# Earlier raw context loads and x loads in the second layer's cross attention of a four-layer transformer

## The chip, the cores and the metric

The kernel runs on 1 core of a Trainium2 chip. The metric is the device time of one execution in microseconds; the median of the runs is what versions are compared by.

## The reference

`x` is (32, 112, 256), `ctx` is (32, 375, 256). Four layers are run one after another on `x`; each attends to the same `ctx`:

```
x = L0(x, ctx)   # x attends to ctx: 16 heads of 64, 4 key heads
x = L1(x, ctx)   # self attention, cross attention, GELU-gated feed-forward
x = L2(x, ctx)   # cross attention with 16 heads of 64, ReLU feed-forward
x = L3(ctx, x)   # causal self attention, cross attention, ReLU feed-forward
```

The second layer's cross attention is what the change touches. It has 16 heads of 16, and its queries, keys, values and attention weights are quantised to 8 bits:

```
h2  = layernorm(x)
q, k, v = h2 @ wq, ctx @ wk, ctx @ wv
sim = einsum(fq(q), fq(k)) * DH**-0.5
out = einsum(fq(softmax(sim)), fq(v))
x   = out @ wo + bo + x
```

## The kernel before, in words

**Sweeps, units and slots.** The work is cut into nine sweeps over the 32 batches: `l0x`, `l1s`, `l1x`, `l1f`, `l2x`, `l2f`, `l3s`, `l3x`, `l3f` (the digit is the layer; s, x and f are self attention, cross attention and feed-forward). Sweeps run in pairs side by side: `l0x` with `l1s`, `l1x` with `l1f`, `l2x` alone, `l2f` with `l3s`, `l3x` with `l3f`. A sweep consists of units; in `l1x` a unit is one batch, and two batches share a layer norm. A unit has slots; in `l1x` eight, each with one pair of heads. `order` merges the slots of all sweeps into one list, and `run` goes through it slot by slot.

**What a slot of `l1x` does.** A slot has steps that come some slots after one another (`LAGS`: 0, 1, 3, 6, 7 for `l1x`). Step 0 makes the scores on TensorE (L1166) and the softmax (`softmax`: maximum L640 on VectorE, scaled maximum L643 and exponential L646 on ScalarE). One slot later the probabilities are scaled and rounded (`quant_p`: L215 on VectorE or GpSimd, L691 on VectorE) into a bf16 tile. Three slots later, in every second slot, a DMA transposes that tile (L1185). Six slots later TensorE multiplies by the values (L1130). Seven slots later, at the last slot of a unit, comes the output projection with the residual sum (L1267).

**Atoms.** Everything else a unit needs is an atom: a piece of work with a lead in slots of its own sweep, a cost on TensorE, and a function. The atoms of a sweep are sorted by the slot they are due in. `settle` runs those without a cost as soon as their slot begins; `fill` spreads those with a cost over the slots before, up to `HORIZON` slots ahead, but never past an atom without a cost that isn't due yet. The leads stand in `LEAD`; a lead of 14 means fourteen slots before the unit's first slot. For `l1x`: `load` and `stats` and `apply` are the load of x, the layer norm's statistics (L460 to L462, L435) and its application (L475, transposes L477); `cload` and `cut` are described next; `q` and `k` are the query and key projections with their quantisation (L213, L949, L970); `apart` spreads queries over heads (L935); `v` makes the values (L1018, L1030); `v2` makes the values of the third layer from the same context and stores them in DRAM as `vd` (L536); `again` loads x a second time for the residual.

**The context in `l1x`.** `ctx_atoms` has two atoms a batch. `load` (`cload`) takes a `k3` tile, has GpSimd clear one column (L574) and issues the DMA of the transposed context, 375 KB (L575). `cut` takes a `k6` tile and splits the raw context into a high and a low part: the copy of the high part goes to ScalarE (L202) and VectorE (L204) in turn, batch by batch, the subtraction to GpSimd (L233). The result is stored as `cd` (L586) for the later sweeps.

**Queues and buffers.** All DMAs are issued by SyncE (SP), in one order. Loads of x (L405), stores of x (L430) and stores of `vd` are held back by `later` and let go by `behind`, right behind the next DMA transpose of `l1x`. Tiles of one tag share a number of buffers: `k3` has 11 (in `l1x`: raw context, probabilities, their bf16 form, its transpose, values, vd tiles), `k6` 5, `x` 11. The instructions that the loop emits are then put in each engine's order when the program is built, by readiness, priority in the order of emission and free buffers; on the chip every engine takes its instructions in that order.

**Beside it.** `l1f` runs in the same stretch, one unit of eight slots for two batches: up projections (L1294), gate shift (L224), GELU on ScalarE (L1311), gating (L1323), down projections (L1334), residual (L866).

Of the kernel before, what the change touches and what calls it, by code (L numbers as in the profile page):

```python
# [61 lines left out]
class Kern:  # L62
# [7 lines left out]
        l1x=[0, 1, 3, 6, 7],  # L70
# [8 lines left out]
    LEAD = dict(  # L79
        l0x=dict(load=11, stats=10, apply=6, cload=11, cstats=8, cut=8, ctrans=5, q=4, k=[2, -2], v=-1),  # L80
        l1s=dict(load=5, stats=5, apply=3, q=2, k=2, v=1),
        l1x=dict(load=17, stats=12, apply=10, cload=14, cut=14, q=8, apart=[2, -1], k=4, v=-1, v2=[-2, -4, -6, -7], again=-7),
        l1f=dict(load=13, stats=11, apply=10, gate=2, gelu=1, again=-3),
        l2x=dict(load=10, stats=7, apply=6, cload=11, cut=7, q=4, k=[1, 1], v=0, vload=2),
        l2f=dict(load=6, stats=5, apply=3),
# [1583 lines left out]
```

## Time and profile before

| | us |
|---|---|
| median of three runs (4796.98, 4806.71, 4807.12) | 4806.71 |
| the profiled execution | 4799.79 |
| its span, first to last instruction | 4797.7 |
| PE busy | 4449.6 (93%) |
| VectorE (DVE) busy | 3619.7 (75%) |
| ScalarE (ACT) busy | 3412.9 (71%) |
| GpSimd (POOL) busy | 2131.3 (44%) |
| mean granted clock of TensorE | 0.968 |
| first and last raw context load of `l1x` | 1090.3 and 2149.5 |

How to read it: PE is TensorE's matrix multiplication, PEld its weight load. A wait row reads "who <- what ended the wait: us in total, times, longest". In the order of time a row gives the start, the duration, the engine, the line, the operation, the tiles out<-in, shapes, and in brackets the idle time of the engine just before, with what ended it. SPq is SyncE's queue of DMA issues; its durations are those of the issue, not of the transfer. Buffer numbers are left out of tile names, so that `k3` and `k6` both read `k`. The windows' columns are the busy time of each engine in that stretch, then the granted clock of TensorE as a share, the busy share of the DMA engines and GB/s.

### The profile page before, as it was taken

To read this page: it belongs to the slowest core of one execution; us is meant where nothing else is said; L and a number is where in the kernel's file an instruction comes from. 1 tells how busy PE (TensorE), PEld (TensorE's weight loads), DVE (VectorE), ACT (ScalarE), POOL (GpSimd) and SP (SyncE) were. 2 spreads that over 40 slices of the span, in tenths; PEclk is the share of its full clock that TensorE was granted. 3 is DMA by queue.
4 is the path that set the end of the run, shared out by engine and by line. 5 is a ranking of instruction groups with operands and counts; after the bars stand their busy time and mean duration, and the time that the engine had idled before them with its cause. 6 is when DMAs were issued, how large, how long until landed. Compare 5 with 4: busy or idle time off the path is not lost.

```text
span 4797.7 us, 111165 instructions
## 1 busy us (share of the span) xinstructions
PE 4449.6 (93%) x37824; PEld 3960.6 (83%) x37824; DVE 3619.7 (75%) x9803; ACT 3412.9 (71%) x10645; POOL 2131.3 (44%) x3676
## 2 busy tenths in 40 slices
PE   7999999998778999999999999999999997899999
PEld 6888888887667888887999999998899986778888
DVE  5788888888888888887688888888566655677776
ACT  5788888887767777775577777775555554677776
POOL 5455455556444343333233333334444443566665
PEclk9999999999889999999999999999999997899999
DMA  4433333334665565566355445543777777666663
GB/s 109 125 87 88 82 86 82 83 84 120 139 132 136 147 144 147 145 153 160 108 144 144 138 140 140 146 142 103 198 218 220 221 201 207 159 165 166 164 166 84
DMA packets 590020, 674.50 MB, mean 141 GB/s; under 512 B 331488, under 2 KB 499664, under 8 KB 589264
## 3 DMA queue, kind: packets, MB, share of 16 engines
q1 hardware_dynamic: 589456, 667.38, 54.6%
q8 instruction: 305, 5.00, 0.5%
q14 instruction: 259, 2.12, 0.1%
HBM read 323.55 MB, written 173.02 MB: 104 GB/s over the span
## 4 chain that ended last, share of the span: by engine, by line
PE 42%; DVE 5%; DMA 4%; ACT 1%; issue 1%; POOL 1%; SPq 0%; ACTq 0%; DVEq 0%; POOLq 0%
PE ps L698 7%; PE ps L237 6%; PE ps L238 5%; PE ps L239 5%; PE sc L807 3%; PE ps L829 3%; PE ps L1130 3%; PE sc L1166 2%; PE acc L237 2%; PE acc L239 1%; PE acc L238 1%; PE ps L1294 1%; DVE sm L640 1%; PE ps L1240 1%; DMA k<-k 1%
## 5 line engine op out<-in xcount | busy, mean ns | idle before, releaser
L219 POOL TENSOR_SCALAR k<-k,sm 112x375 f32<-112x375 f32 (+1 forms) x1536 | 941.7, 626 | 1054.1 <-DVE sm L680 474.5
L202 ACT ACTIVATE k<-ps 125x336 f32<-125x336 f32 (+4 forms) x2005 | 916.3, 470 | 419.8 <-PE ps L239 185.2
L640 DVE TENSOR_REDUCE sm<-sc 112x1 f32<-112x375 f32 x1792 | 945.1, 539 | 150.7 <-PE sc L807 86.6
L646 ACT ACTIVATE k<-sc,sm 112x375 f32<-112x375 f32 x1536 | 881.9, 580 | 103.3 <-DVE sm L640 79.9
L698 PE MATMUL ps<-ident,k 112*125 112x112 f32 x4608 | 736.4, 278 | 20.4 <-issue 4.0
L698 PEld LDWEIGHTS ps<-ident,k 112*125 112x125 f32 x4608 | 653.5, 191 | 76.0 <-issue 45.7
L807 PE MATMUL sc<-k,qs 128*112 128x376 f32 x2048 | 540.7, 357 | 21.4 <-ACT k L646 11.4
L237 PE MATMUL ps<-w,k 128*125 128x256 f32 (+2 forms) x1344 | 426.3, 317 | 32.0 <-ACT k L646 17.4
L729 DVE TENSOR_TENSOR k<-ps,k 64x376 fp32r<-64x376 f32 x640 | 350.3, 547 | 121.7 <-ACT k L202 106.5
L237 PE MATMUL ps<-h,w 128*128 128x224 f32 x1408 | 408.8, 297 | 34.6 <-DVE h L204 13.0
L204 DVE COPY k<-ps 125x336 f32<-125x336 f32 (+2 forms) x619 | 289.7, 468 | 152.3 <-PE ps L239 60.2
L238 PE MATMUL ps<-h,w 128*128 128x224 f32 x1408 | 394.0, 282 | 2.6 <-POOL h L233 2.0
L239 PE MATMUL ps<-h,w 128*128 128x224 f32 x1408 | 393.2, 282 | 1.3 <-POOL w L233 1.2
L238 PE MATMUL ps<-w,k 128*125 128x256 f32 (+2 forms) x1344 | 385.6, 287 | 0.0
L239 PE MATMUL ps<-w,k 128*125 128x256 f32 (+2 forms) x1344 | 384.7, 286 | 0.0
L829 PE MATMUL ps<-k,k 125*64 125x112 f32 (+1 forms) x4608 | 351.9, 297 | 1.6 <-ACT k L202 1.3
L215 POOL TENSOR_SCALAR k<-k,sm 112x375 f32<-112x375 f32 x256 | 165.8, 648 | 416.8 <-DVE sm L680 314.9
L237 PE MATMUL ps<-k,w 128*128 128x376 f32 x896 | 336.5, 376 | 15.2 <-ACT k L646 5.8
L807 PEld LDWEIGHTS sc<-k,qs 128*112 128x112 f32 x2048 | 305.3, 177 | 50.7 <-ACT k L646 24.9
L237 PEld LDWEIGHTS ps<-w,k 128*125 128x125 f32 (+2 forms) x1344 | 258.8, 193 | 82.5 <-ACT k L646 30.3
L646 ACT ACTIVATION_READ_ACCUMULATOR k<-sc,sm 112x1 f32 x1536 | 323.7, 211 | 0.0
L237 PEld LDWEIGHTS ps<-h,w 128*128 128x128 f32 x1408 | 272.4, 197 | 56.8 <-issue 18.2
(216 smaller groups left out, 12559.6 us busy)
## 6 DMA issues: line engine op xcount, KB each, us to landing
qs<-h SPq DMA_DIRECT2D x512, 224.0 KB
k<-k SPq DMA_DIRECT2D x192, 376.0 KB
k<-cd SPq DMA_DIRECT2D x64, 752.0 KB
vd<-k SPq DMA_DIRECT2D x128, 375.0 KB
k<-vd SPq DMA_DIRECT2D x128, 375.0 KB
qs<-dq_l3s SPq DMA_DIRECT2D x128, 224.0 KB
qs<-dq_l3x SPq DMA_DIRECT2D x128, 224.0 KB
x<-xd SPq DMA_DIRECT2D x224, 112.0 KB
```

What stands on the lines that cost most here:

```text
L202: self.nc.scalar.activation(out, in_, AF.Identity)
L204: self.nc.vector.tensor_copy(out, in_)
L219: self.nc.gpsimd.tensor_scalar(out, in_, by, 1.0, ALU.mult, ALU.mult)
L237: mm(out, lhs(0), rhs(0), start=start, stop=False)
L238: mm(out, lhs(0), rhs(1), start=False, stop=False)
L239: mm(out, lhs(1), rhs(0), start=False, stop=stop)
L640: nc.vector.tensor_reduce(nms[j], sc[j][:, :n], AX.X, ALU.max, negate=True)
L646: nc.scalar.activation(p[:, j, :n], sc[j][:, :n], AF.Exp, bias=nms[j], scale=1.0 if scale is None else scale, accum_out=sm[:, j : j + 1])
L698: self.nc.tensor.transpose(pst[:TB, a * S : (a + 1) * S], p[:, j, a * TB : (a + 1) * TB], self.ident[:S, :S])
L729: nc.vector.tensor_tensor(ks[o, j, :], pk[r, :TE], ks[r, j, :].bitcast(F32), ALU.subtract)
L807: nc.tensor.matmul(sc[:, :TE], qs[:, hd, q, bs], kk, start=q == 0, stop=q == 1)
L829: nc.tensor.matmul(o if gqa else o[:, mm, :], vq[:, a, hd * 64 : hd * 64 + 64], st["pt"][:, :, j, ta] if gqa else st["pt", mm][:, j, ta], ...
```

## The change

Two leads of `l1x` are altered. The load of x is emitted 20 slots ahead of its unit and not 17, its statistics still 12 slots ahead. The load of the raw context is emitted 16 slots ahead and not 14, while its split stays at 14, so that the two no longer fall in the same slot. No operation is added or removed.

```
     LEAD = dict(
         ...
-        l1x=dict(load=17, stats=12, apply=10, cload=14, cut=14, q=8, apart=[2, -1], k=4, v=-1, v2=[-2, -4, -6, -7], again=-7),
+        l1x=dict(load=20, stats=12, apply=10, cload=16, cut=14, q=8, apart=[2, -1], k=4, v=-1, v2=[-2, -4, -6, -7], again=-7),
```

## The prediction

> **What bounds the kernel now.** I read the page first, then the busy times by stage, then the raw context load with its waiters, then the order of time around one split. All numbers are of the profiled execution: 4799.79 us, span 4797.7 us, so 2.1 us lie around the span. The median of the runs shown is 4806.71 us, 6.9 us above it.
>
> ```profile
> span 4797.7 us, 111165 instructions
> PE 4449.6 (93%) x37824; PEld 3960.6 (83%) x37824; DVE 3619.7 (75%) x9803; ACT 3412.9 (71%) x10645; POOL 2131.3 (44%) x3676
> ...
> PE   7999999998778999999999999999999997899999
> ...
> PEclk9999999999889999999999999999999997899999
> ```
>
> PE is the engine nearest its limit, and it is loosest, with a lowered clock, in slices 10 to 13 (about 1080 to 1560 us). That is where `l1x` begins beside the tail of `l1s`. The raw loads (L575) run from 1090.3 to 2149.5 us, one a batch, some 33 us apart in the steady part, so a slot of `l1x` is about 4.2 us there. Only this stage is touched. Its first part, its steady part, and then 13 us around the split of an even and of an odd batch, in turn, three times:
>
> ```profile
> 1090.00:1500.00 410.00, 326.63 (x2446) 269.50 (x2445) 346.44 (x966) 298.58 (x903) 193.67 (x335) 0.86 0.59 132
> 1500.00:2160.00 660.00, 609.49 (x4643) 533.25 (x4642) 552.72 (x1517) 501.81 (x1360) 255.15 (x394) 0.98 0.61 147
> 1727.00:1740.00 13.00, 9.38 (x66) 7.73 (x66) 9.95 (x30) 7.14 (x16) 3.91 (x6) 0.87 0.77 169
> 1761.00:1774.00 13.00, 12.43 (x96) 10.12 (x95) 10.30 (x29) 9.48 (x29) 6.28 (x8) 1.00 0.63 168
> 1793.00:1806.00 13.00, 10.38 (x73) 8.70 (x72) 10.69 (x32) 8.29 (x17) 4.52 (x6) 0.87 0.74 178
> 1827.00:1840.00 13.00, 13.00 (x103) 11.34 (x102) 10.02 (x29) 9.73 (x29) 6.13 (x8) 1.00 0.62 161
> 1591.00:1604.00 13.00, 10.21 (x71) 8.64 (x70) 8.87 (x25) 7.56 (x18) 3.81 (x5) 0.84 0.86 194
> 1627.00:1640.00 13.00, 12.99 (x103) 11.50 (x102) 10.22 (x31) 10.10 (x30) 6.41 (x8) 1.00 0.59 161
> ```
>
> The columns are PE, PEld, DVE, ACT and POOL busy, granted clock, DMA share and GB/s. In the even windows PE is idle for 3.62, 2.62 and 2.79 us at a clock of 0.84 to 0.87; in the odd ones for 0.57, 0 and 0.01 us at full clock. Something happens every second batch. The split's first half falls on ACT in even and on DVE in odd batches, and this is who waits for the raw load in the whole run (us, times):
>
> ```profile
>   ACT k L202: 24.6, 13
>   DVE k L204: 5.3, 5
>   POOL k L215: 2.7, 1
> ```
>
> One even batch in order of time:
>
> ```profile
> 1724.43 0.80 SPq L575 DMA_DIRECT2D k<-in_ctxT_dram  x1
> 1728.61 1.91 SPq L1185 DMA_TRANSPOSE k<-k  x1
> 1730.72 0.83 ACT L202 ACTIVATE k<-k 128x752 fp32r<-128x752 f32 x1 [3.32 <-DMA k<-in_ctxT_dram]
> 1732.14 1.53 DVE L949 TENSOR_SCALAR ki<-ki 128x376 f32<-128x376 f32 x1 [2.49 <-ACT ki L213]
> 1734.61 0.30 ACT L643 ACTIVATE sm<-sm,sc 112x2 f32<-112x2 f32 x1 [2.51 <-DVE sm L640]
> 1735.51 1.07 PE L1294 MATMUL ps<-h,w 128*128 128x224 f32 x4 [2.59 <-ACT ki L213]
> ```
>
> The load is issued at 1724.43, behind a vd store and a run of seven x loads. ACT reaches the split at 1727.40 and stands for 3.32 us. The key quantisation (L213) queued behind it is late, DVE stands for 2.49 us on that, the softmax maximum is late for ACT (2.51 us), and PE stands for 2.59 us. The split's own consumer is some ten slots away: all of this is one instruction at the head of a queue.
>
> **The change, part by part.** *Raw load, 14 to 16.* Same count: 32 memsets on POOL (median 0.10 us) and 32 loads. Each load is emitted 2 x 4.2 = 8.4 us earlier, moved on SP past one transpose and one vd store, and on POOL past one or two scalings. In the batch shown SP issues nothing from 1711.05 to 1716.61, so there is room for its 0.4 us. Issue to use was 6.3 us in the batch shown; with 8.4 us more the load has landed before ACT arrives. Its transfer now lies ahead of another transpose than before. The nearest price for that is the 2.1 us between 1728.61, when the transpose went after its wait on the vd store, and 1730.72, when the raw load was there; but the transpose it now burdens is outside the x burst, and the one it leaves gains the same, so I take zero, with a bound of a PE wait like those that PE has on the transposes, 4.4 us in 6 waits in the steady part.
>
> *First term, the stalls.* All waits on the raw load sum to 24.6 + 5.3 + 2.7 = 32.6 us. The end can win at most this, and nothing if each stall is covered by another wait. In the steady part the stalls are 16.4 + 2.9 + 2.7 = 22.0 us, and PE waits on the key quantisation there, L1294 for L213, for 11.6 us in 6 waits: 0.53 of it. GELU (L1311: 1.28 us table load and 1.70 us) falls into the same even batches and remains, so I take half: 16.3 us.
>
> *Second term, the clock.* In 1736.40 to 1739.80 the granted clock is 0.50 with PE busy for 3.40 of 3.40 us, 0.9 us after the 2.59 us gap. The steady part's loss is 660 x 0.02 = 13.2 us, and ten even windows at 13 x 0.14 = 1.8 us would hold 18, so it sits next to these stalls. Early, 410 x 0.14 = 57 us are lost, mostly to the many other waits there; a quarter, 14 us, is the most I would give to its three ACT stalls (8.2 us). So the bounds are 0 and 27 us; I take half of the steady loss and little of the early one, 8 us, because half of the gaps should stay.
>
> The Trainium skill's page "TensorE: Matmul & The Clock Gate", Part 1, has the clock halve after an idle window of about 3.4 us. No gap shown here is that long, so by that rule the second term would be zero and the sum 16.3 us. The row at 1736.40 shows half clock after 2.59 us, and the row decides.
>
> *x loads, 17 to 20.* 32 issues of about 0.42 us, flushed behind a transpose three slots earlier. For the batch pair loaded at 1721.6 the statistics read x at 1736.2, more than ten us after its issue. The only long waits on x (DVE L460, 9.2 us in 2) are of the feed-forward's own first loads near 1438 and 1476 us, so nothing is won directly. Taking two of seven loads from the burst frees about 0.8 us of SP ahead of the raw load. Three to five of eleven x buffers are in use on the mean in the steady part. Zero, with up to 5 us either way from the order of the queue.
>
> *Buffers.* The raw tile shares the eleven `k3` buffers with probabilities, their quantised and transposed forms, value tiles and vd tiles; it lived 11.4 us (median) and will live some 20. Following each tile from first write to last read or landing, I count two to four free buffers in the eight us before the present raw load, and none or one in the last five us before the split. The added time falls on the first stretch, so I take zero; the other end is the second rival.
>
> Sum: 16.3 + 8 = 24.3 us off 4799.8, 4775.5; on the scale of the median 6.9 more, 4782.4, or 4783.
>
> **The rivals.** *The wait moves (no change).* GELU, transposes and vd stores sit in the same even batch. If PE meets one of them as late, only stalls with no such neighbour count. For it: PE also waits there on transposes (DMA k<-k, 4.4 us in 6) and on exponentials (L1166 for L646, 5.2 us in 6). Against it: the chain above starts at the split and has no other late link. Gain about 5 us, within 9.6 us: 0.2% of 4806.7 is 9.6 us, about what a measurement of this kernel can tell from no change. Time about 4802.
>
> *Buffer shortage (slower).* With one `k3` buffer gone for 8.4 of every 33 us, transposes and exponentials take buffers that have only just been given up, and wait for a store to land. For it: SP's transposes already wait 103.5 us in 21 waits on vd stores in the steady part, and ACT, DVE and POOL for 4.9 us in 7. Against it: the free buffers counted. Price: 8.4/33 of one in eleven is 2.3%, of the stage's 1060 us 24 us; or, if every batch gains one wait as long as PE's longest on a transpose in the steady part (1.1 us), 32 x 1.1 = 35 us. It decides once no buffer is free in the two slots before the old load: 4807 + 24 to 35, 4831 to 4842.
>
> *The load is not issued earlier.* The order of SP is set when the program is scheduled; if the load stays where it is, nothing changes. The idle stretch of SP speaks against it; it is counted with no change.
>
> **How the numbers follow.** Forecast case 0.60, no change 0.15, shortage 0.25. Within the forecast case the bounds 0 to 59 us are ends, and most of it lies between 4760 and 4796. The range takes that in and reaches into the shortage: 4750 (57 us off) to 4835. On its own the likeliest case has 4760 to 4796. Chances: faster by over 0.2% 0.60, within 0.15, slower 0.25.
>
> **What would show it.** Right: no ACT or DVE wait on the raw load; even windows with PE idle near 1.5 us and a clock above 0.93; L575 ahead of the x loads; the stage from first to last raw load shorter by some 24 us, everything after l1x unchanged. Wrong: the even windows keep their 3 us of PE idle, now ended by GELU's neighbours or transposes (no change); or waits of exponentials and transposes on vd stores grow, with the odd windows showing idle too (shortage).

## The result and the profile after

The kernel after takes 4814.58 us (median of 20 runs, 4804.27 to 4822.67), the kernel before 4804.28 us on the same chip (20 runs, 4796.94 to 4815.97). The ratio is 1.0021, 95% interval [1.0014, 1.0028]: some 10 us slower, where the forecast was 24 us faster. The profiled execution of after took 4819.61 us with a span of 4817.8 us. It lies 20 us above the profiled execution of before, twice the difference of the medians: about half of the loss that the views below show belongs to these two executions and not to the change.

The page of after, the rows that answer to those shown of before:

```profile
span 4817.8 us, 111247 instructions
...
PE 4447.5 (92%) x37824; PEld 3957.1 (82%) x37824; DVE 3633.6 (75%) x9803; ACT 3408.4 (71%) x10645; POOL 2138.4 (44%) x3676
...
PE   7999999998778999999999999999999997899999
...
PEclk9999999999889999999999999999999998899999
```

PE's work is the same to 2 us, so the 20 us of span are PE standing idle. The waiters for the raw context load, in the whole run of after:

```profile
  ACT k L202: 14.7, 9
  DVE k L204: 5.0, 6
```

That is 19.7 us where before had 32.6: the stalls that the change aimed at became fewer, but stayed. Busy times by stretch, first the two parts of the stage, with the columns as before:

```profile
1090.00:1500.00 410.00, 311.89 (x2378) 258.94 (x2378) 345.72 (x941) 291.73 (x885) 192.16 (x332) 0.89 0.54 130
1500.00:2160.00 660.00, 605.72 (x4582) 527.38 (x4582) 549.98 (x1500) 494.01 (x1344) 260.35 (x386) 0.98 0.63 143
```

The count in brackets is the best measure of progress in a fixed stretch: PE did 2378 + 4582 = 6960 matmuls where before did 2446 + 4643 = 7089, although its granted clock was higher in the first part (0.89, before 0.86). At before's pace the 129 missing ones are 129 x 1070 / 7089 = 19 us. The last transpose of `l1x` (L1185) is issued at 2260.2 us, before at 2243.0, so that in this pair of executions 17 of the 20 us are lost by the end of the `l1x` stage.

One pair of batches shows where such a loss can stand. The stretch from one even split to the next, in five pieces, first of before (its first piece, 1727 to 1740, is among the lines of the prediction), then of after:

```profile
1740.00:1753.00 13.00, 12.28 (x104) 10.64 (x103) 10.68 (x32) 10.95 (x29) 3.61 (x7) 1.00 0.39 102
1753.00:1766.00 13.00, 13.00 (x88) 11.53 (x87) 11.83 (x34) 10.47 (x32) 7.78 (x10) 1.00 0.55 131
1766.00:1780.00 14.00, 13.43 (x107) 11.64 (x106) 11.42 (x32) 10.76 (x31) 5.93 (x9) 1.00 0.67 169
1780.00:1793.00 13.00, 13.00 (x112) 12.10 (x111) 9.81 (x32) 10.65 (x32) 4.38 (x9) 1.00 0.67 167
```

```profile
1725.00:1738.00 13.00, 12.80 (x102) 10.75 (x101) 12.20 (x30) 10.41 (x31) 7.29 (x11) 1.00 0.73 199
1738.00:1751.00 13.00, 10.04 (x71) 8.56 (x70) 8.94 (x30) 7.43 (x17) 2.16 (x5) 0.87 0.91 145
1751.00:1764.00 13.00, 11.58 (x99) 10.01 (x97) 10.32 (x30) 10.88 (x27) 3.61 (x8) 1.00 0.34 82
1764.00:1778.00 14.00, 12.06 (x89) 10.33 (x79) 12.60 (x32) 9.75 (x30) 9.60 (x9) 1.00 0.60 159
1778.00:1792.00 14.00, 14.00 (x112) 12.70 (x112) 11.84 (x32) 12.07 (x35) 4.80 (x8) 1.00 0.62 134
```

The window around the split is cured: 0.20 us idle at full clock, where before lost 3.62 us at 0.87. But the loss stands 13 us later: 2.96 us idle, and again a clock of 0.87. Before idles 4.91 us in the 66 us of this pair, after 6.52 us in 67 us. The cure is not this batch's alone: in the 13 us around the split (from 3.3 us ahead of it) PE idles 22.8 us in sum over the ten even batches of the steady part in before, and 10.8 us in after. Over the steady part as a whole, 1500 to 2160 us, its idle time did not fall: 50.5 us in before and 54.3 us in after. The order of time of after in this stretch:

```profile
1725.20 0.41 SPq L575 DMA_DIRECT2D k<-in_ctxT_dram  x1
1729.08 0.84 ACT L202 ACTIVATE k<-k 128x752 fp32r<-128x752 f32 x1 [0.41 <-DMA k<-in_ctxT_dram]
...
1734.71 5.55 SPq L1185 DMA_TRANSPOSE k<-k  x1
...
1742.37 4.44 SPq L1185 DMA_TRANSPOSE k<-k  x1
1745.54 0.21 PE L1130 MATMUL ps<-k,k 128*32 128x112 bf16 x1 [2.96 <-DMA k<-k]
```

The split follows its load by 3.9 us; before had 6.3 us (1724.43 to 1730.72). Over all 32 batches the median from issue to split is 6.0 us, in before 6.7. PE now stands for a transpose. It went at 1734.71, as soon as its own input was there (L691 on VectorE, 1734.12 to 1734.67), but its issue took 5.55 us, where the median of the 128 is 1.38. SP's waits from 1732 to 1746 us are these:

```profile
SPq L1185 <- DVE sm L461: 6.5, 1, 6.5
SPq L1185 <- PE ps L1130: 4.0, 1, 4.0
```

The first line must not be read as a wait for the layer norm's statistics (L461). Of VectorE's instructions this transpose needs L691 alone, by the program; where an issue is long, the view puts it down to whatever VectorE finished last before the issue's end. Why the issue is long isn't shown. It stands behind five x loads and three stores, and the DMA engines are busiest in the piece that follows (0.91); but before has one of 4.87 us as well, at 1733.93 us, and no such gap of PE behind it. The second line is a wait for a buffer: the next transpose needs a tile that PE frees with the very matrix multiplications that stood (L1130).

### The profile page after: what moved, and what is told of

The parts are those of the page before. It is cut to its first block, busy times and chain, and to the rows that moved or that the text cites. A ratio compares the mean times of both kernels' runs of the same rounds, so it can differ in the third digit from the quotient of the medians.

```text
span 4817.8 us, 111247 instructions
## 1 busy us (share of the span) xinstructions
PE 4447.5 (92%) x37824; PEld 3957.1 (82%) x37824; DVE 3633.6 (75%) x9803; ACT 3408.4 (71%) x10645; POOL 2138.4 (44%) x3676
## 5 line engine op out<-in xcount | busy, mean ns | idle before, releaser
L237 PEld LDWEIGHTS ps<-h,w 128*128 128x128 f32 x1408 | 274.0, 198 | 59.1 <-issue 19.7
```

Of the source, the lines that this page charges most:

```text
L237: mm(out, lhs(0), rhs(0), start=start, stop=False)
```

## The experiments

All ratios are against before on the same chip, from five rounds, with the 95% interval. "Order" means the order in which the engines issue their instructions, compared in the built programs; an instruction that isn't in the common sequence counts as moved. The counts in the expectations come from matching blocks of the two orders and are upper bounds. The longest common sequence of line, operation and tiles in the two traces moves fewer, on ACT and DVE: 75 and 233 with the constant below (80 and 258 in its expectation), and for the x loads at 16, 18, 19 and 20 slots 23 and 54, 92 and 197, 431 and 944, 97 and 205. Counts outside the expectations are of this second kind.

**One half of the change each.** Only the raw load earlier, and only the x loads earlier:

```
e1_cload16   l1x=dict(load=17, ... cload=16, cut=14, ...)
e1_load20    l1x=dict(load=20, ... cload=14, cut=14, ...)
```

> Only the raw context load moves, to 16 slots ahead; x stays at 17. Theory A (the split follows its load): in the program's order the load goes one transpose earlier on SP and the split six exponentials earlier on ACT, so the wait on the raw load stays at 15 to 25 us, and the loss of the change belongs to this part: 1.0015 to 1.003 of the kernel before, about 4812 to 4818 us. Theory B (the x loads' burst, moved behind the raw load, is the loss): 0.998 to 1.000, as the shorter wait then counts alone.

> Only the x loads move, to 20 slots ahead; the raw load stays at 14. Theory A: no difference that can be measured, 0.999 to 1.001, with the wait on the raw load at 28 to 36 us as before. Theory B: the loss belongs here, 1.002 to 1.003.

Measured: 4810.81 us, 1.0016 [1.0006, 1.0026], and 4828.34 us, 1.0049 [1.0033, 1.0065]. Neither half is a gain. The x loads alone cost more than the whole change (1.0021) and more than either theory allowed, so the two halves don't add up. In e1_cload16 ACT and DVE still wait 12.2 and 3.1 us for the raw load. The order says why: `cut=14` held nothing back. On SP the last raw load stands behind 114 of the transposes of `l1x` instead of 115, and the last split stands six exponentials earlier on ACT and four maxima earlier on DVE. The split moved with its load. When the program is built, an instruction is placed once its data are expected; a load that comes earlier pulls its reader ahead, and the distance between the two hardly grows.

**The split held in its place.** The same, with the copy of the high half kept behind the last softmax maximum and exponential emitted before it:

```
+            with self.tc.issue_after(self.pins[0].ins), self.tc.issue_after(self.pins[1].ins):
+                self.copy("ctx", o[:, :, 0, :], c["raw"])
```

> The changed kernel, with the split's copy ordered behind the last softmax maximum and exponential that were emitted before it, so that it can't be put in ACT's or DVE's order ahead of its slot. The load stays one transpose earlier. Theory A, with the stalls worth half their length: the wait on the raw load falls below 6 us and the time to 0.995 to 0.998 of the kernel before (4780 to 4795 us). Rival (the stalls have cover from other waits, worth nothing): the wait falls as well, the time is 0.999 to 1.003.

> As the pinned kernel, with x at 17 as before the change. Theory A: wait on the raw load below 6 us, 0.995 to 0.998, equal to the pinned kernel with x at 20 within 0.001. Theory B: faster than that one by 0.002 or more, as the x loads stay where they were. Rival (stalls worth nothing): 0.999 to 1.001.

Measured: 4812.20 us, 1.0015 [1.0002, 1.0027] with both halves of the change, and 4813.95 us, 1.0024 [1.0014, 1.0034] with the raw load alone. In the first, the view of the raw load lists no waiter at all (in the second one, of 0.7 us):

```profile
L576 SPq DMA_DIRECT2D k<-in_ctxT_dram x32: 383/409/1287, 1089.0 to 2159.0; - x32
its engine sat idle before it (us, times) until:
who waited for it (us, times):
busy tenths in 40 slices 0000000000000000000000000000000000000000
```

This is the kernel that the prediction had in mind, all 32.6 us of stalls gone, and it isn't faster. Its order isn't that of before, though, so it doesn't price the stalls alone. The second lies above the 0.999 to 1.001 that its rival had allowed.

**The stall by itself.** Before, with the high half copied from a constant, held in place as above. The low half, on GpSimd, is still the raw context minus the high one. Few instructions move (75 on ACT, 233 on DVE):

```
-            self.split(c["raw"], o[:, :, 0, :], o[:, :, 1, :], ("ctx", "crest"))
+                self.copy("ctx", o[:, :, 0, :], self.nhalf[:, :2].unsqueeze(2).to_broadcast([128, 2, TE]))
```

> The kernel before, with the high half of the split copied from a constant and not from the raw context (so the split is no longer an exact one; the low half, on GpSimd, still reads the raw context and waits for it), held at its slot. Of the other instructions 80 of 7619 on ACT and 258 of 9805 on DVE change their place. Theory C (a stall of ACT or DVE here is worth nothing, since TensorE meets another wait as late): no ACT or DVE wait on the raw load, 0.999 to 1.002 of the kernel before. Theory A (the stalls are worth half their length, and what the changed kernels lose is in the orders that come along): 0.995 to 0.998.

Measured: 4810.01 us, 1.0009 [1.0001, 1.0018]. ACT and DVE no longer wait; GpSimd does:

```profile
  POOL k L586: 79.3, 24
```

Its subtraction stood 66.1 us in sum in before too, mostly for the copy of the high half; here it stands 83.7 us. So this run takes the stalls from ACT and DVE, and not from GpSimd.

What PE waited for longest from 1666 to 2260 us, one line each of before, of after and of e2_stale:

```profile
PE ps L1294 <- ACT ki L213: 9.6, 6, 2.6
```

```profile
PE ps L1294 <- ACT k L646: 11.5, 10, 2.0
```

```profile
PE ps L478 <- DVE ot L1149: 9.3, 3, 3.3
```

The wait on the key quantisation, the end of the predicted chain, is gone in the other two (1.0 us in 3 in each). In its place PE waits as long for the exponentials (after) or for the low part of the attention's output (e2_stale). In sum PE's idle time from 1500 to 2160 us is larger in e2_stale too, 62.5 us, where before has 50.5.

**The series of leads.** If a lead acts through one mechanism, the time should follow it; if it acts by putting the instructions in another order, it should scatter. X loads at 16, 18 and 19, and the raw load at 18, 15 and 13 (13 with its split):

> Only the x loads move, to 16 slots ahead: behind the same transpose as with 17, 155 of ACT's and 59 of DVE's instructions elsewhere. Theories D and E alike: 0.999 to 1.001. If it is off by more than 0.002 either way, small changes of order alone are worth as much as the change studied.

> Only the x loads move, to 18 slots ahead: one transpose earlier on SP, where 20 slots are two. ACT's and DVE's orders differ from the kernel before in nearly the same instructions as with 20 slots (506 and 775 moved, against 505 and 763). Theory D (the loss with 20 slots is in those orders): 1.003 to 1.007, as with 20. Theory E (the loss is in where the x loads lie among the transposes): 0.999 to 1.003.

> Kernel before with the x loads 19 slots ahead (raw load at 14). Theory 'the x loads cost by which transpose they stand behind': like 18 and 20 slots, 0.2 to 0.5 per cent slower. Rival 'it is the order of the other engines that changes by chance': anywhere from 0.3 per cent faster to 0.5 per cent slower, with no trend over 16, 18, 19 and 20 slots.

> Only the raw load moves, to 18 slots ahead: two transposes earlier on SP; the split goes ten exponentials earlier on ACT than before the change (956 instead of 966 at the last), once more with the load. Theory A (the split follows its load): the wait on the raw load stays at 10 to 25 us and the time at 1.001 to 1.004. Rival (two slots were too few for the landing): wait below 6 us, time 0.995 to 0.999.

> Kernel before with the raw load one slot earlier (cload=15, x loads at 17). Theory 'the split follows its load and the waits on the raw load are covered': within 0.2 per cent of before, or slower by as much as with two slots (0.16 per cent). Rival 'one slot is enough to take the stalls away and the loss comes from going further': 8 to 16 us faster.

> Kernel before with the raw load and its split both one slot later (cload=13, cut=13; x loads as before). Theory 'earlier loads pull the split ahead and that is what costs': a later one costs nothing, 0 to 8 us faster. Rival 'each step away from the present order costs, whichever way': 4 to 15 us slower, with stalls on the raw load as long as before (about 33 us).

| x loads, raw load at 14 | ratio | raw load, x loads at 17 | ratio |
|---|---|---|---|
| 16 | 1.0005 [0.9997, 1.0014] | 13 | 1.0183 [1.0169, 1.0197] |
| 17 | before | 14 | before |
| 18 | 1.0020 [1.0009, 1.0031] | 15 | 1.0032 [1.0019, 1.0045] |
| 19 | 0.9984 [0.9970, 0.9998] | 16 | 1.0016 [1.0006, 1.0026] |
| 20 | 1.0049 [1.0033, 1.0065] | 18 | 1.0045 [1.0031, 1.0059] |

The x loads show no trend: 19 slots are a little faster than before, 20 slots the slowest of the five. Nothing in `l1x` waits for their data in any of the five: VectorE's waits on x loads in the stage, 8 to 14 us, are those of the feed-forward's own. Load 18 meets theory E and misses theory D: the traces of load 18 and load 20 differ in only 9 ACT, 33 DVE and 6 GpSimd instructions, and in 33 on SP, and yet the two stand at 1.0020 and 1.0049. So what load 20 loses beyond load 18 hardly lies in ACT's and DVE's orders; where the x loads stand on SP is the likelier place, but load 19, between the two, gains, and no run settles it. Load 19 moves the most instructions and is the fastest, so their number doesn't tell the time. With it, 4798.39 us, there is a version faster than before by 0.16% [0.02, 0.30]; as the best of many tried, it may owe part of that to luck.

Of the places tried for the raw load, 14 is the best; at 18 slots both the loss and the waits on the load (30.3 us) are above theory A's range, and neither theory took in the loss at 15 or at 13. One slot later costs 84 us, and there the waits are long and most of them are DVE's:

```profile
  DVE k L204: 44.3, 15
  ACT k L202: 26.7, 12
```

**Is GELU the neighbour?** The second guess was that GELU, in the same even batches, covers the stalls. Three kernels without it (before, before with the constant high half, after):

```
-            u.atoms.append((L["gelu"], 0, lambda: nc.scalar.activation(g["g"], g["g"], AF.Gelu)))
```

> Kernel before without the GELU of the feed-forward beside the cross attention (the gate goes on without it, so that part of the reference isn't computed): 16 activations of 1.70 us and the table loads of 1.28 us around them are gone from ScalarE. Theory 'GELU is the neighbour that covers the stalls': PE loses its 3 us gaps in even batches, time shorter by 16 x 1 to 3 us, 16 to 48 us, about 4765. Rival 'PE is held by many small waits of equal size': the time moves by under 10 us, as with the stalls on the raw context.

> As e3_nogelu, and the high half of the raw context made from a constant and held in place, so that ScalarE and VectorE never wait for the raw load (what is left out: GELU, and the context's high half in the second layer's cross attention). It is read against e3_nogelu. Theory 'GELU covers the stalls': now that GELU is gone, taking the stalls away is worth something, 8 to 16 us less than e3_nogelu. Rival 'many small waits of equal size': within 10 us of e3_nogelu, either side.

> The kernel after without that GELU (left out as in e3_nogelu), read against e3_nogelu. If what the change costs comes from how its new order stands around GELU, its 0.2 per cent are gone: equal to e3_nogelu or faster. If it comes from the x loads among the transposes or from the order at large, it stays 5 to 20 us slower than e3_nogelu.

Measured: 0.9974 [0.9965, 0.9983], 1.0008 [0.9999, 1.0017] and 1.0004 [0.9995, 1.0013]. Taking 31 us of work off ACT (3412.9 to 3382.3 us busy) gave 13 us, between the two theories, and in the profiled executions none of it in this stage: the last transpose of `l1x` is at 2250.1 us, before at 2243.0. Without GELU the constant high half is again slower than its own base, 1.0008 against 0.9974, and so is the change. So nothing here shows GELU covering the stalls. This reading is weaker than the others, since without GELU the order is another throughout, and the 14 us by which the constant makes it slower are more than the 10 us that the rival allowed.

**No reader of the raw load.** e3_c13 left open whether long stalls cost after all. First its high half was made constant as in e2_stale:

> As e3_c13 (raw load and split one slot later), and the high half of the raw context made from a constant and held in place, so that ScalarE and VectorE never wait for the raw load; the low half on GpSimd still reads it (what is left out: the context's high half in the second layer's cross attention). It is read against e3_c13, 4890 us and 71 us of waits on the raw load. Theory 'a stall on the raw load costs once it is long enough': most of the loss goes, 4805 to 4835. Rival 'the stalls are worth nothing here too, the order costs': it stays above 4865.

Measured: 4877.92 us, 1.0150 [1.0135, 1.0165]. Of 84 us only 12 are won. But GpSimd now waits 108.2 us for the raw load, and quantisations stand behind it. So in the last three kernels the low half comes from the constant too, and the load is issued but read by nobody, in orders close to those of before, of after and of e3_c13:

```
+            self.eng("crest").tensor_tensor(o[:, :, 1, :], self.nhalf[:, :2].unsqueeze(2).to_broadcast([128, 2, TE]), o[:, :, 0, :].bitcast(F32), ALU.subtract)
```

> Kernel before with both halves of the context in the second layer's cross attention made from a constant and the copy held in place: the raw load is issued as before, and no engine reads it (left out: the context itself in that attention and in what is stored as cd). No stall on the raw load is left on any engine. Theory 'the stalls are worth nothing in before': within 0.2 per cent of before. Rival 'they were worth half, and the waits of GpSimd took the gain in e2_stale': 12 to 25 us faster than before.

> The same edit on the kernel after; read against e5_full. Theory 'the loss of the change is that of another order of instructions': it stays 5 to 20 us slower than e5_full. Rival 'the loss goes by the raw load and its waits': equal to e5_full within 5 us.

> The same edit on e3_c13 (raw load and split one slot later); read against e3_c13, e4_c13_stale and e5_full. Theory 'the order costs': above 4860, near e4_c13_stale's 4878. Rival 'waits on the raw load cost, on GpSimd too once they are long': 4800 to 4835.

| | as it is | no reader of the raw load |
|---|---|---|
| before | 1 | 0.9988 [0.9979, 0.9997] |
| after | 1.0021 [1.0014, 1.0028] | 0.9969 [0.9956, 0.9981] |
| e3_c13 | 1.0183 [1.0169, 1.0197] | 1.0039 [1.0027, 1.0051] |

This is the nearest measure of the first term: with no reader of the raw load left, before gains 6 us, and the interval reaches to 10. It also speaks against the simplest account of the loss, "another order is a worse order": in after's order the gain is 0.52%, 25 us, and the kernel ends below before's. And in e3_c13 most of the loss seems to go by the raw load. These differences still hold some scatter of order, since taking the reader away moves 95 ACT instructions in before, 121 in after and 93 in e3_c13.

One pair is free of that, and it shows that what of the raw load costs so much is not settled. e1_pin_after and e5_full_after have the same order on all five engines: only the 32 copies and 32 subtractions read another tile. Nobody waits for the raw load in either; yet they stand at 1.0015 [1.0002, 1.0027] and 0.9969 [0.9956, 0.9981]. Three things differ: the raw tile gives its `k3` buffer back when the load has landed, not after the subtraction (the tile's life falls from 13.8 to 5.6 us, median, estimated from the semaphores); the subtraction is shorter; and the numbers that go on from there are constants. First e1_pin_after's group, then e5_full_after's, mean in ns after the comma:

```profile
L586 POOL TENSOR_TENSOR k<-k,k 128x752 fp32r<-128x752 f32 x32 | 58.0, 1813 | 2.5 <-ACT k L203 1.5 <-POOL k L216 0.7
```

```profile
L586 POOL TENSOR_TENSOR k<-nhalf,k 128x752 fp32r<-128x752 f32 x32 | 46.8, 1461 | 2.9 <-ACT k L203 2.0 <-DVE k L205 0.7
```

GpSimd has 11 us less to do, and VectorE's instructions, the same in both, take 9 us less in sum (1171.1 and 1162.1 us in the stage, in the profiled executions). SP's waits of the raw load for a buffer are as long in both, so these are not what the pair differs by:

```profile
SPq L576 <- DMA k<-k: 43.1, 23, 3.7
```

```profile
SPq L576 <- DMA k<-k: 42.0, 23, 3.8
```

No run here separates the three. But 0.46% came without any change of order, so the 10 us that the change lost can't simply be put down to order.

## Why the prediction was wrong, step by step

Why the gain did not come is shown by the runs. Why the kernel became 10 us slower stays open.

**The stall and its chain** were read rightly in the batch that was shown: after has neither the 3.32 us at the split nor the 2.59 us gap of PE, and the even window runs at full clock. The raw load stands ahead of the x loads there, as named, and the ten even batches of the steady part improved as well (22.8 to 10.8 us of PE idle around the split). But the stage was to become 24 us shorter, and from first to last raw load it takes 1068.6 us, before 1059.2: the step from the stall to the time was wrong.

**"The load has landed before ACT arrives"** failed first. Earlier emission moved the load past one transpose on SP, as said, but the split moved with it, since its lead of 14 holds nothing back: issue to split was to grow by 8.4 us, and its median went from 6.7 to 6.0. That left 19.7 of 32.6 us. I named a rival in which the load stays where it is, and none in which its reader comes along.

**The first term, 16.3 us for half the stalls,** is the step that failed and decides. Taken away alone, the stalls of ACT and DVE bring no gain (e2_stale, 1.0009 [1.0001, 1.0018]); together with GpSimd's and with the buffer given back early, 6 us. The ratio of 0.53 was PE's wait on the quantisation over the stalls. It says how long PE waited there, not what PE would save: in after and in e2_stale this wait went, and another of about the same length stood in its place.

**The second term, 8 us of clock,** brought nothing. In the profiled executions the granted clock rose from 0.968 to 0.971, in 1090 to 1500 us from 0.86 to 0.89, but PE did fewer matmuls there; over all runs the median is 0.968 in before and 0.969 in after.

**The x loads, zero with up to 5 us either way,** were mis-sized: 2, 10, -8 and 24 us at 16, 18, 19 and 20 slots, worked out as the ratio times 4803 us. The 5 us were given to the order of SP's queue. What a lead does to the orders of all engines was not priced, and it can be five times as much. How much of the 24 us is in the whole change, which loses 10, isn't known.

**Buffers, zero.** In the stage, SP's waits of the raw load for a buffer just given up by a transpose rose from 5.7 us in 13 to 37.2 us in 22, and transposes wait for buffers that PE still reads 15.5 us in 8 instead of 4.4 in 5. So the buffers are tighter, and the zero was too low for these waits. That they set the time isn't shown: the transpose behind the 2.96 us gap above stood for its input and a long issue, not for a buffer, and in e1_pin_after the transposes' wait is back to 2.9 us, and nothing is won.

**The rivals.** "The wait moves" has the mechanism that the runs show for the stalls, and its time was too good by the cost of the rest: 1.0021 lies at the edge of the 0.2% it allowed. "Buffer shortage" has the sign, and some of its marks, but its 24 to 35 us are two to three and a half times the loss, and that it is the cause is not established.

## What to carry to other kernels

The worth of a stall isn't its length, nor the length of the wait that it causes on the busiest engine, when that engine has many waits of the same size: measure it by feeding the stalled instruction from data that are always there, with the order held. A lead that is moved alters the order of everything behind it, so run its neighbours too; here five leads of a load whose data nothing in its sweep waits for spread over 0.65%, three times the effect of the change. And in a fixed stretch compare the counts of matmuls, not the busy share.

## What was not expected of the hardware

**The same copy on VectorE takes 0.54 or 1.5 us.** The split's copy of 128x752, in before, in after and in e1_pin_after (mean in ns after the comma):

```profile
L204 DVE CAST k<-k 128x752 fp32r<-128x752 f32 x16 | 8.7, 545 | 5.3 <-DMA k<-in_ctxT_dram 5.3
```

```profile
L204 DVE CAST k<-k 128x752 fp32r<-128x752 f32 x16 | 12.0, 748 | 5.0 <-DMA k<-in_ctxT_dram 5.0
```

```profile
L205 DVE CAST k<-k 128x752 fp32r<-128x752 f32 x16 | 15.5, 968 | 0.0
```

In before all 16 take 0.54 or 0.55 us, and 15 of them have no GpSimd instruction beside them. In e1_pin_after seven take 1.50 us, each with GpSimd at work from its start to its end, while seven others beside GpSimd take 0.53 or 0.54; in after four take 0.89 to 1.97 us. One of each kind in e1_pin_after:

```profile
1760.99 1.84 POOL L938 TENSOR_TENSOR pp<-ot,ownb 128x896 bf16<-128x896 bf16 x1 [0.28 <-PE ps L240]
1761.73 1.50 DVE L205 CAST k<-k 128x752 fp32r<-128x752 f32 x1
```

```profile
1901.28 1.71 POOL L216 TENSOR_SCALAR k<-k,sm 112x375 f32<-112x375 f32 x1 [0.58 <-DVE sm L683]
1901.55 0.53 DVE L205 CAST k<-k 128x752 fp32r<-128x752 f32 x1
```

The Trainium skill's page "SBUF — State Buffer", section "SBUF: two separate sides", has VectorE and GpSimd share a pair of ports that whichever instruction starts first holds to its end; on VectorE this is for instructions in a two-port mode or with two inputs there. The late copies agree with that: all seven begin 0.74 to 0.81 us into the same GpSimd instruction, a multiplication of two tiles (L938), and end 0.4 us after it. The seven untouched ones don't sort by who started first, as far as the profile's rough GpSimd spans tell: they begin 0.09 to 0.38 us into a GpSimd instruction with one tile to read, and aren't held. Which of the two differences decides, the kind or the lead, wasn't tested. The cost is small here: 16 x 0.42 = 7 us of VectorE over the stage.

**Half the clock after a gap of under 3 us.** After shows it more plainly than the row of the prediction, where PE was busy for 2.78 us only of the 6.40 us ahead of the low clock. Here PE stands once, for the 2.96 us that end at 1745.54, and from 1746.40 to 1749.80 the granted clock is 0.50 with PE busy all the time. The 13 us window of it has 0.87, and its neighbours have 1.00. Of the gaps of 2.6 to 3.0 us, four of five in before and six of six in after are followed by a lower clock.
